# Routing of layer 1's mixture of experts in smaller chunks: eight tiles for the first four, more pieces behind a block, five sends

## The chip, the cores and the metric

The kernel runs on one core of a Trainium2 chip. The metric is the device time of one execution in microseconds; the time before is the median of 3 runs. The core has five engines with queues of their own, each working in order: PE (matmul, with its weight loads shown as PEld), DVE (vector), ACT (activations), POOL (GpSimd) and SP, which here only issues DMAs. POOL issues DMAs too, among them the indirect ones that this change is about.

## The reference, cut to what matters

Four layers, each an attention-like block and a feed-forward block, on 32 x 256 tokens of width 128, that is 8192 tokens, or 64 tiles of 128 tokens. The change lies in layer 1. Its first half is a linear attention with a causal mask; its second half a mixture of eight experts:

```python
x = x + _L1_attn_ref(_layernorm(x), ...)   # q, k, v, gate; elu + 1; causal (q k^T) v / (q . cumsum k)
xf = _layernorm(x).reshape(-1, 128)
logits = xf @ gate_w + gate_b                # (8192, 8)
top_w, top_i = jax.lax.top_k(logits, 2)
gw = softmax(top_w)
out = sum over e of combine[:, e] * (gelu(xf @ w1[e] + b1[e]) @ w2[e] + b2[e])
shared = gelu(xf @ ws1 + bs1) @ ws2 + bs2
x = x + out + shared
```

## The kernel before, in words

The residual stream `K.x` stays in on-chip memory as 64 tiles (`NT`), and a block is four tiles, so there are 16 blocks (`NBLK`). Each token has to reach the two experts that it chose. The kernel does this by sending: the class `Slots` keeps, in device memory, a list of rows for each expert (`f_rows`); every token's normalised row goes, with its return address and its weight, to a slot of the list of its first expert and once more to a slot of its second. Afterwards `S.experts` walks over the lists in groups of 256 rows, fetches a group (`xs<-f_rows`), applies that group's expert and scatters the results back (`f_back`). It can fetch the first group only when all sends have landed.

One send is one indirect DMA from POOL (`S.send`, L478): 128 rows of 130 numbers, one tile for one of the two choices, 128 sends in all. Just before it, DVE casts the tile's slot numbers to integers (`one`, L1422). There are eight buffers of `one`, so a cast waits until the send eight places earlier has landed.

Before a tile can be sent it goes through routing, in chunks of tiles (16 before the change):

- `settle` (L1316): once the attention of the chunk's tiles is done, the mean and the inverse root of the variance are worked out by DVE in small steps (`Norm.steps`, L258 to L300, then L1322), and ACT writes the normalised rows into `row` (L1327), one instruction a tile.
- `gate` (L1333): block by block, PE transposes four tiles of `row`, ACT copies them to `xnT` (L1353), PE multiplies by `gate_w` (L1348), and DVE adds the bias into `logits` (L1359).
- `choose` (L1366): DVE picks the two best experts of each token (L1384 to L1395), ACT takes an exponential, and `Slots.places` works out the slot: the picks are counted by two matmuls (L403 and L404) and one running sum along the tiles of each expert (`tensor_tensor_scan`, L408), whose mask `go_on` starts anew at each expert. At the end two lists of sends are queued in `outgoing`, those of the first choice and those of the second, and between them `second`, which has POOL rewrite the return addresses (L373) and weights (L1417) of the chunk's rows.

`settle` and `choose` are generators: every `yield` ends a piece of one or two instructions. `beside(n, most)` is the call that weaves them in. It issues up to `most` entries of `outgoing` (`send`), runs one `gate`, and then n times advances every active generator by a piece; of the `choose` generators only the first in line advances.

`beside` is called at the end of each round of two loops. The attention's loop has 21 rounds for 16 blocks, in six stages: in round n block n-5 is in `third`, n-4 in `second`, n-3 in `keys`, n-2 in `first`, n-1 in `turn` and n in `scale`; here the call is `beside(10, 5)`. A chunk's `settle` becomes active in the round in which its last block has been through `third`. The shared expert's loop has 17 rounds (`rise`, L1592 and L1596, then `fall` of the block before, L1601, L1607 and L1613), with `beside(14, 4)`. After it everything left in `outgoing` is sent, `S.finish` numbers the groups (L440 to L469), and `S.experts` starts. The experts' weights (`w_all`) are loaded by SP between the two loops.

In both loops the order on PE, ACT and DVE is the order of the program text (`manual_schedule`); POOL's order is left to the scheduler. POOL's other work in the attention is one addition a block (`q+qr`, L1513), whose result `second` reads two rounds later.

The lines in the lists below are those of the kernel before.

Of the kernel before, what the change touches and what calls it, by code (L numbers as in the profile page):

```python
# [11 lines left out]
F32 = mybir.dt.float32  # L12
# [3 lines left out]
ALU = mybir.AluOpType  # L16
# [4 lines left out]
P = 128  # L21
NB, SEQ, D = 32, 256, 128
NT = NB * SEQ // P
# [280 lines left out]
class Slots:  # L304
# [8 lines left out]
    GROUP, WIDE, NE = 256, D + 2, 8  # L313
# [22 lines left out]
            )  # L336
            nc.gpsimd.dma_start(rows[i], t)  # L337

    def begin(self, pool, most):

        nc = self.K.nc
        self.every = pool.tile([P, P], BF16, name="every")
        self.first = pool.tile([P, P], BF16, name="first")
        nc.gpsimd.memset(self.every, 1.0)
        nc.gpsimd.affine_select(
            out=self.first, in_=self.every, pattern=[[1, P]], compare_op=ALU.is_gt, fill=0.0,
            base=0, channel_multiplier=-1,
        )
        self.go_on = pool.tile([P, self.NE, most], F32, name="go_on")
        nc.gpsimd.memset(self.go_on, 1.0)  # L350
        nc.gpsimd.memset(self.go_on[:, :, 0:1], 0.0)
        self.seen = pool.tile([P, self.NE], F32, name="seen")
        self.floor = pool.tile([P, self.NE], F32, name="floor")
        for t in (self.seen, self.floor):
            nc.gpsimd.iota(
                t, pattern=[[self.ROOM, self.NE]], base=0, channel_multiplier=0,
                allow_small_or_imprecise_dtypes=True,
            )
        n = NT * P // self.GROUP
        self.steps = pool.tile([P, n], F32, name="steps")  # L360
# [17 lines left out]
    def places(self, pool, bank, picks, out):  # L378


        NE = self.NE
        nc = self.K.nc
        n, most = picks[0].shape[1], self.go_on.shape[2]

        def new(name, dtype=F32):
            return pool.tile([P, NE * most], dtype, name=name)[:, 0 : NE * n]

        taken = new("taken", BF16).rearrange("p (e n) -> p e n", e=NE)
        turned = [m.rearrange("p n e -> p e n") for m in picks]
        if len(picks) == 1:  # L390
            nc.vector.tensor_copy(taken, turned[0])
        else:
            nc.vector.tensor_add(taken, *turned)
        yield

        yield "PE"
        t = bank()
        before, total = (
            (t[:, i, 0 : NE * n] if len(t.shape) == 3 else t[:, i * NE * n : (i + 1) * NE * n])
            .rearrange("p (e n) -> p e n", e=NE)  # L400
            for i in range(2)
        )
        nc.tensor.matmul(before, self.first, taken, start=True, stop=True)  # L403
        nc.tensor.matmul(total, self.every, taken, start=True, stop=True)  # L404

        sums = new("sums").rearrange("p (e n) -> p e n", e=NE)
        if n == most:
            nc.vector.tensor_tensor_scan(  # L408
                sums.rearrange("p e n -> p (e n)"), self.go_on.rearrange("p e n -> p (e n)"),
                total.rearrange("p e n -> p (e n)"), 0.0, ALU.mult, ALU.add,  # L410
            )
        else:
            for e in range(NE):
                nc.vector.tensor_tensor_scan(
                    sums[:, e, :], self.go_on[:, e, 0:n], total[:, e, :], 0.0, ALU.mult, ALU.add
                )
        slot = new("slot").rearrange("p (e n) -> p e n", e=NE)
        nc.vector.tensor_sub(slot, sums, total)
        nc.vector.tensor_add(slot, slot, before)
        yield  # L420
        nc.vector.tensor_add(slot, slot, self.seen.unsqueeze(2).to_broadcast([P, NE, n]))
        nc.vector.tensor_add(self.seen, self.seen, sums[:, :, n - 1])
        yield
        for m, u in zip(picks, out):
            mine = new("mine").rearrange("p (n e) -> p n e", e=NE)
            s = pool.tile([P, most], F32, name="place")[:, 0:n]
            nc.vector.tensor_mul(mine, m, slot.rearrange("p e n -> p n e"))
            yield
            nc.vector.tensor_reduce(s, mine, axis=AX.X, op=ALU.add)
            yield  # L430
            nc.vector.tensor_copy(u, s)
            yield
# [820 lines left out]
def layer1(K):  # L1253
# [1 line left out]

    nc, ins = K.nc, K.ins
    NE, F = 8, 512
    FC, CHUNK = F // P, 16
    LONG = 2 * F + FC + D
    S = K.slots1  # L1260
    before, after = K.norm_of_x, K.next_norm()
# [10 lines left out]
    with ExitStack() as es:  # L1272
# [13 lines left out]
        gate_b = K.load_bcast(sp, "f1_gate_b", NE)  # L1286
        shared = sp.tile([P, LONG], F32, name="shared")
        numbers(shared, NE, nc.sync)
        S.begin(sp, CHUNK)
        order = sp.tile([P, NE], F32, name="order")  # L1290
        nc.gpsimd.iota(
            order, pattern=[[-1, NE]], base=NE, channel_multiplier=0,
# [22 lines left out]
        active, ready, turned, logits, hold, outgoing = [], [], [], {}, {}, []  # L1315
        slot_of = [rw.tile([P, NT], F32, name=f"slot{i}") for i in range(2)]  # L1316

        def settle(lo):
            hi = lo + CHUNK
            for _ in after.steps(lo, hi):  # L1320
                yield
            nc.vector.scalar_tensor_tensor(  # L1322
                nmr[:, lo:hi], after.mean[:, lo:hi], -1.0, after.r[:, lo:hi], ALU.mult, ALU.mult
            )
            yield
            for j in range(lo, hi):
                nc.scalar.activation(  # L1327
                    row[:, j, 0:D], K.x[:, j, :], AF.Identity, bias=nmr[:, j : j + 1],
                    scale=after.r[:, j : j + 1],
                )  # L1330
                if j % 4 == 3:
                    ready.append(j // 4)
                yield  # L1333

        def gate():

            count = [g for g in active if hold.get(g[1])][:1]
            new = ready.pop(0) if ready else None
# [13 lines left out]
            if new is not None:  # L1352
                nc.scalar.copy(xnT[:, new, :], t)  # L1353
                turned.append(new)
            if old is not None:
                lo, at = 4 * old // CHUNK * CHUNK, 4 * old % CHUNK
                if at == 0:
                    logits[lo] = lw.tile([P, CHUNK, NE], F32, name="lg")
                nc.vector.tensor_add(  # L1359
                    logits[lo][:, at : at + 4, :], out,  # L1360
                    gate_b.unsqueeze(1).to_broadcast([P, 4, NE]),
                )
                if at == CHUNK - 4:
                    active.append((choose(lo), lo))
            for g in count:
                hold[g[1]] = u[:, 256:512]  # L1366
                go(g)

        def choose(lo):
            n, hi = CHUNK, lo + CHUNK  # L1370
            lg = logits.pop(lo)

            def new(name, *shape):
                return rw.tile([P, n, *shape], F32, name=name)

            def wide(t):
                return t.unsqueeze(2).to_broadcast([P, n, NE])
# [87 lines left out]
        with ExitStack() as at:  # L1465
# [79 lines left out]
            def third(blk):  # L1545
# [18 lines left out]
                        ALU.mult, ALU.add,  # L1564
                    )
                after.take(K.x, 4 * blk, 4 * blk + 4)
                if (4 * blk + 4) % CHUNK == 0:
                    active.append((settle(4 * blk + 4 - CHUNK), None))

            with K.tc.manual_schedule(  # L1570
                engines={nc.tensor.engine, nc.scalar.engine, nc.vector.engine}
            ):
                stages = [(5, third), (4, second), (3, keys), (2, first), (1, turn), (0, scale)]
                for n in range(NBLK + 5):
                    for later, stage in stages:
                        if 0 <= n - later < NBLK:
                            stage(n - later)
                    beside(10, 5)


        w_all = K.pool(es, "l1a", 1).tile([P, NE, LONG], F32, name="w_all")
# [2 lines left out]
        with ExitStack() as ps:  # L1584
# [30 lines left out]
            with K.tc.manual_schedule(  # L1615
                engines={nc.tensor.engine, nc.scalar.engine, nc.vector.engine}
            ):
                for n in range(NBLK + 1):
                    if n < NBLK:
                        rise(n)  # L1620
                    if n:
                        fall(n - 1)
                    beside(14, 4)
                assert not (active or ready or turned)
                send(len(outgoing))
                nc.scalar.copy(w_all[:, :, 2 * F + FC :], b2[:, 0:NE, :])
# [1152 lines left out]
```

## Time and profile before

| What | us |
|---|---|
| median of 3 runs (lowest to highest) | 3095.63 (3092.87 to 3099.08) |
| the profiled execution: time / span | 3072.12 / 3070.4 |
| layer 1, attention's rounds with all engines at work | 871 to 991 of the span |
| shared expert's rounds | 991 to 1123 |
| from the last matmul of the shared expert to the first of the experts | 1123 to 1205 |

The profile shows one execution. "Busy" is the time in which an engine had an instruction; an idle engine's waits are named by what ended them. In a list of windows each row is a stretch of the span with the busy time and the number of instructions of each engine, then the clock that PE was granted (1.00 is full) and the share and rate of the DMA engines. In a timeline a row is the start in us, the duration, the engine, line and operation, the output and inputs, and in brackets the idle time before it with what ended it.

### The profile page before, as it was taken

What the parts mean: (1) busy time and instruction counts of PE and PEld (TensorE: products, weight loads), DVE (VectorE), ACT (ScalarE), POOL (GpSimd) and SP (SyncE); (2) the same over time, 40 slices, a digit from 0 to 9 for tenths busy, and PEclk for the clock granted to TensorE, in tenths of its full rate; (3) what the DMA queues carried; (4) which work ended last, traced back from release to release, by engine and by line L of the source; (5) the groups of instructions that cost most, each with busy time, mean ns of one, the idle gap of its engine ahead of it and who ended that gap; (6) DMA issues with size and microseconds to landing.
All of it is one profiled execution on the core that took longest, in us unless ns stands there. A gap on an engine that the chain in (4) does not pass through costs nothing.

```text
span 3070.4 us, 59293 instructions
## 1 busy us (share of the span) xinstructions
PE 2481.3 (81%) x21486; PEld 1840.0 (60%) x21486; DVE 1853.4 (60%) x5498; ACT 1426.3 (46%) x3065; POOL 853.9 (28%) x1235
## 2 busy tenths in 40 slices
PE   4899787899889962999488888996978888887470
PEld 4865444444857742999466667775855555555460
DVE  7215454444878312444379766764869988886447
ACT  3433432222468521444435555556427677776223
POOL 1001444310012455455310101100520223343573
PEclk9999789999989986999779989997979999999795
DMA  2497455540000211222455434430034445451334
GB/s 72 141 283 223 173 231 228 217 152 21 12 1 13 82 40 52 70 70 70 117 155 160 128 113 141 132 95 13 1 86 137 128 125 143 130 147 42 91 91 112
DMA packets 263264, 340.81 MB, mean 111 GB/s; under 512 B 34598, under 2 KB 231062, under 8 KB 254780
## 3 DMA queue, kind: packets, MB, share of 16 engines
q1 hardware_dynamic: 231228, 237.01, 27.1%
q0 software_dynamic: 27584, 97.92, 8.5%
q8 instruction: 170, 2.79, 0.4%
q10 hardware_dynamic: 4160, 2.10, 0.3%
q14 instruction: 122, 1.00, 0.1%
HBM read 156.72 MB, written 177.83 MB: 109 GB/s over the span
## 4 chain that ended last, share of the span: by engine, by line
PE 39%; DVE 12%; DMA 7%; issue 5%; ACT 5%; POOL 4%; SPq 1%; DVEq 0%; POOLq 0%; ACTq 0%
PE o L1909 5%; PE t L1888 5%; DVE top L1845 4%; PE o L557 4%; PE hp L538 4%; DMA q<-row 4%; PE s L1784 2%; PE s L1833 2%; POOL f_back L484 2%; PE d L1607 2%; PE a L1592 2%; ACT e L1896 2%; DMA f_rows<-row,one 2%; DVE st_x L246 1%; PE a L1492 1%
## 5 line engine op out<-in xcount | busy, mean ns | idle before, releaser
L1845 DVE TENSOR_REDUCE top<-s 128x3 f32<-128x384 f32 (+1 forms) x1024 | 600.5, 617 | 189.5 <-PE s L1742 133.3
L1896 ACT ACTIVATE e<-t 128x384 f32<-128x384 f32 (+1 forms) x1024 | 494.0, 546 | 128.2 <-PE s L1742 82.7
L1888 PE MATMUL t<-q,k 64*128 64x256 f32 (+1 forms) x2048 | 417.1, 308 | 115.8 <-ACT e L1896 60.9
L1833 PE MATMUL s<-k,q 48*128 48x256 f32 (+1 forms) x2048 | 437.8, 331 | 30.3 <-DMA k<-d 16.7
L1888 PEld LDWEIGHTS t<-q,k 64*128 64x128 f32 x2048 | 299.7, 191 | 194.8 <-ACT e L1896 90.2
L1833 PEld LDWEIGHTS s<-k,q 48*128 48x128 f32 x2048 | 308.2, 198 | 43.6 <-DVE top L1845 23.9
L544 ACT ACTIVATE h<-hp,w 128x256 f32<-128x256 f32 x368 | 154.6, 471 | 332.8 <-PE hp L538 324.0
L484 POOL DMA_INDIRECT f_back<-y,place x224 | 217.4, 970 | 191.8 <-DVE y L563 125.8
L1909 PE MATMUL o<-e,val 128*32 128x256 f32 (+1 forms) x4096 | 262.0, 376 | 0.0
L538 PE MATMUL hp<-xT,w 128*128 128x256 f32 x736 | 184.4, 390 | 20.4 <-DVE xT L529 20.3
L557 PE MATMUL o<-w,h 128*128 128x128 f32 x1472 | 183.4, 276 | 0.0
L2079 POOL TENSOR_SCALAR xn<-x_sb,mean_x,r_x 128x128 f32<-128x128 f32 x64 | 55.2, 871 | 449.4 <-PE t L1773 394.0
L557 PEld LDWEIGHTS o<-w,h 128*128 128x128 f32 x1472 | 174.0, 193 | 1.5
L1909 PEld LDWEIGHTS o<-e,val 128*32 128x32 f32 x4096 | 110.7, 113 | 81.8 <-issue 12.8
L538 PEld LDWEIGHTS hp<-xT,w 128*128 128x128 f32 x736 | 133.4, 194 | 40.8 <-DVE xT L529 26.4
L1742 PE MATMUL s<-hideq,pick 64*128 64x128 bf16 x1024 | 151.6, 233 | 0.0
L478 POOL DMA_INDIRECT f_rows<-row,one x128 | 123.4, 964 | 94.2 <-DVE one L1422 61.7
L1742 PE MATMUL t<-hidek,pick 64*128 64x128 bf16 x1024 | 147.3, 227 | 0.0
L527 PE MATMUL t<-ident,xs 128*128 128x128 f32 x224 | 43.9, 278 | 101.4 <-DMA xs<-f_rows 101.4
L563 DVE TENSOR_TENSOR y<-o,xs 128x256 f32<-128x256 f32 x112 | 47.3, 422 | 114.2 <-PE o L557 113.9
L337 POOL DMA_DIRECT2D f_rows<-blank x176 | 98.3, 559 | 54.5 <-POOL blank L333 51.2
L775 PE MATMUL up<-wc,hT 128*128 128x128 f32 x768 | 110.8, 297 | 0.0
(522 smaller groups left out, 5294.8 us busy)
## 6 DMA issues: line engine op xcount, KB each, us to landing
f_rows<-blank POOLq DMA_DIRECT2D x176, 390.0 KB, 2.8
tz<-kpad SPq DMA_DIRECT2D x64, 512.0 KB
d<-high SPq DMA_DIRECT2D x128, 256.0 KB
d<-low SPq DMA_DIRECT2D x128, 256.0 KB
q<-d SPq DMA_DIRECT2D x128, 256.0 KB
k<-d SPq DMA_DIRECT2D x128, 256.0 KB
xs<-f_rows SPq DMA_DIRECT2D x112, 130.0 KB
t<-f_back SPq DMA_DIRECT2D x24, 512.0 KB
```

Source lines behind the costliest of these rows:

```text
L478: i = self.K.nc.gpsimd.indirect_dma_start(self.rows, bass.IndirectOffsetOnAxis(ap=slot, axis=0), row, None)
L484: i = self.K.nc.gpsimd.indirect_dma_start(self.back, bass.IndirectOffsetOnAxis(ap=place, axis=0), row, None)
L538: nc.tensor.matmul(hp[:, i, :], w[:, (c + i) * P : (c + i + 1) * P], xT, start=True, stop=True,)
L544: nc.scalar.activation(h[:, c + i, :], hp[:, i, :], act, bias=w[:, b1 : b1 + 1])
L557: nc.tensor.matmul(o[:, i, :], h[:, c, i * P : (i + 1) * P], w[:, F + c * D : F + c * D + D], start=False, stop=i == N - 1 and c == FC - 1,)
L775: nc.tensor.matmul(o, hT[:, 2 * blk + b, s : s + P], wc[:, j, cs], start=j == 0, stop=False)
L1742: nc.tensor.matmul(t.rearrange("p (n q) -> p n q", n=3)[:, 0:3:2, 64 * n : 64 * n + 64], pick[r, n, :], hide[name][r], start=False, stop=n ...
L1833: nc.tensor.matmul(s[:, lo:hi], q[r, p, h * P : (h + 1) * P], k[r, p, 0 : hi - lo], start=h == 0, stop=not causal and h == 1,)
L1845: nc.vector.tensor_reduce(tops[b][:, :, j, p], out_of["s"][:, 0:used].rearrange("q (h k) -> q h k", h=3 if causal else 2), axis=AX.X, op=A ...
L1888: nc.tensor.matmul(t[:, kh * SEQ : kh * SEQ + SEQ - skip], k[r, p, kh * P : (kh + 1) * P], q[r, p, skip:SEQ], start=kh == 0, stop=not caus ...
L1896: nc.scalar.activation(e, t, AF.Exp)
L1909: nc.tensor.matmul(o[32 * i : 32 * i + 32, skip:SEQ], val[b % RING][:, kh, 4 * m + i, 16 * s : 16 * s + 32], e[:, kh * SEQ : kh * SEQ + SE ...
```

## The change

`CHUNKS` takes the place of a fixed `CHUNK`: four chunks of 8 tiles and two of 16. `settle`, `choose` and the bookkeeping of `gate` go by the chunk that a tile belongs to. `Slots.begin` builds a mask `go_on` for each size in use, so that `places` can do one running sum for both sizes. The attention's rounds call `beside(18, 5)` in place of `beside(10, 5)`, and the shared expert's `beside(14, 5)` in place of `beside(14, 4)`. Layer 3 calls `Slots` with a single size, 8, and keeps it.

```diff
-    def begin(self, pool, most):
+    def begin(self, pool, *sizes):
...
-        self.go_on = pool.tile([P, self.NE, most], F32, name="go_on")
-        nc.gpsimd.memset(self.go_on, 1.0)
-        nc.gpsimd.memset(self.go_on[:, :, 0:1], 0.0)
+        self.go_on = {}
+        for n in sizes:
+            go_on = self.go_on[n] = pool.tile([P, self.NE, n], F32, name=f"go_on{n}")
+            nc.gpsimd.memset(go_on, 1.0)
+            nc.gpsimd.memset(go_on[:, :, 0:1], 0.0)
...
-        if n == most:
-            nc.vector.tensor_tensor_scan(
-                sums.rearrange("p e n -> p (e n)"), self.go_on.rearrange("p e n -> p (e n)"),
-                total.rearrange("p e n -> p (e n)"), 0.0, ALU.mult, ALU.add,
-            )
-        else:
-            for e in range(NE):
-                nc.vector.tensor_tensor_scan(
-                    sums[:, e, :], self.go_on[:, e, 0:n], total[:, e, :], 0.0, ALU.mult, ALU.add
-                )
+        nc.vector.tensor_tensor_scan(
+            sums.rearrange("p e n -> p (e n)"), self.go_on[n].rearrange("p e n -> p (e n)"),
+            total.rearrange("p e n -> p (e n)"), 0.0, ALU.mult, ALU.add,
+        )
...
-    FC, CHUNK = F // P, 16
+    FC = F // P
+
+    CHUNKS = [range(lo, lo + 8) for lo in (0, 8, 16, 24)] + [range(32, 48), range(48, NT)]
...
-        S.begin(sp, CHUNK)
+        S.begin(sp, *sorted({len(c) for c in CHUNKS}))
...
+        def chunk_of(j):
+            return next(c for c in CHUNKS if j in c)
+
-        def settle(lo):
-            hi = lo + CHUNK
+        def settle(c):
+            lo, hi = c.start, c.stop
...
-                lo, at = 4 * old // CHUNK * CHUNK, 4 * old % CHUNK
+                c = chunk_of(4 * old)
+                lo, at = c.start, 4 * old - c.start
...
-                if at == CHUNK - 4:
-                    active.append((choose(lo), lo))
+                if at == len(c) - 4:
+                    active.append((choose(c), lo))
...
-                if (4 * blk + 4) % CHUNK == 0:
-                    active.append((settle(4 * blk + 4 - CHUNK), None))
+                c = chunk_of(4 * blk)
+                if 4 * blk + 4 == c.stop:
+                    active.append((settle(c), None))
...
-                    beside(10, 5)
+                    beside(18, 5)
...
-                    beside(14, 4)
+                    beside(14, 5)
```

More of the change, by code (lines that the diff above doesn't have):

```diff
@@ L382, in places @@
         nc = self.K.nc
-        n, most = picks[0].shape[1], self.go_on.shape[2]
+        n, most = picks[0].shape[1], max(self.go_on)
         def new(name, dtype=F32):
@@ L1355, in gate @@
             if old is not None:
-                lo, at = 4 * old // CHUNK * CHUNK, 4 * old % CHUNK
+                c = chunk_of(4 * old)
+                lo, at = c.start, 4 * old - c.start
                 if at == 0:
-                    logits[lo] = lw.tile([P, CHUNK, NE], F32, name="lg")
+                    logits[lo] = lw.tile([P, 16, NE], F32, name="lg")
                 nc.vector.tensor_add(
@@ L1367, in gate, with choose @@
                 go(g)
-        def choose(lo):
-            n, hi = CHUNK, lo + CHUNK
-            lg = logits.pop(lo)
+        def choose(c):
+            lo, hi, n = c.start, c.stop, len(c)
+            lg = logits.pop(lo)[:, 0:n, :]
             def new(name, *shape):
-                return rw.tile([P, n, *shape], F32, name=name)
+                return rw.tile([P, 16, *shape], F32, name=name)[:, 0:n]
             def wide(t):
```

## The prediction

> **What bounds the kernel now.** I read the page's chain first (it names TensorE, PE, for 39% of the span, spread over the whole kernel), then cut layer 1 into stretches. The columns are the stretch, its length, busy time of PE, PEld, DVE, ACT and POOL, granted clock, DMA share and GB/s.
>
> ```profile
> 877.00:985.00 108.00, 103.61 (x617) 80.66 (x616) 96.18 (x348) 91.06 (x170) 18.83 (x14) 0.98 0.00 1
> 1006.50:1123.40 116.90, 116.62 (x713) 87.86 (x711) 29.05 (x133) 54.16 (x86) 54.40 (x60) 1.00 0.15 47
> 1123.40:1202.70 79.30, 0.02 (x1) 0.00 (x0) 14.26 (x72) 0.00 (x0) 56.29 (x63) 0.53 0.15 50
> ```
>
> The first stretch is the attention, where PE, DVE and ACT are all nearly full and POOL has 14 instructions. The second is the shared expert, bound by PE. In the third nothing runs but sends. The waits of that stretch say who pays:
>
> ```profile
> PE t L527 <- DMA xs<-f_rows: 81.7, 1, 81.7
> DVE one L1422 <- DMA f_rows<-row,one: 60.4, 51, 3.3
> ```
>
> PE stands for 81.7 us until the first group of rows can be fetched, which needs every send landed. POOL's timeline prices a send:
>
> ```profile
> 1177.85 0.96 POOL L478 DMA_INDIRECT f_rows<-row,one  x1 [0.30 <-issue]
> 1180.45 0.16 POOL L373 IOTA row<- 128x16 f32 x1 [1.64 <-DMA f_rows<-row,one]
> 1180.54 0.20 POOL L1417 COPY row<-weight 128x16 f32<-128x16 f32 x1
> 1181.23 1.00 POOL L478 DMA_INDIRECT f_rows<-row,one  x1 [0.49 <-POOL row L1417]
> 1182.53 0.96 POOL L478 DMA_INDIRECT f_rows<-row,one  x1 [0.30 <-issue]
> ```
>
> One send every 1.26 us (0.96 + 0.30). The relabelling of the rows for the second choice (`second`, L373 and L1417) waits for sends in flight: 3.38 us from send to send, 3.59 at the other place in this tail, thus 2.2 more than a plain step.
>
> **How many sends go where.** Unrolling both programs (a round is one call of `beside`; rounds 0 to 20 belong to the attention, then 17 to the shared expert): before, 10 sends go out in rounds 19 and 20, 62 in the shared rounds up to the last but one, 56 from the last on. After: 42 in rounds 12 to 20 (5, 4, 5, 5, 5, 4, 5, 5, 4), 77 in the first sixteen shared rounds, 5 in the last and 4 left over, so 9 at the end.
>
> **The tail.** Before, the 56 start from 1126.24 to 1200.28: 53 x 1.263 + 3.59 + 3.38 = 73.9, shown 74.04. After, the last but one round's five may start where its four did (1121.19), the nine follow, and the last starts at 1121.19 + 13 x 1.263 = 1137.6. That is 62.7 us earlier. The expert numbering on DVE (L440 to L469: 1192.48 to 1199.96, 7.5 us) then has less to hide behind: the last cast waits for the ninth send from the end (start 1127.5, landed about 3.3 later), so the numbering ends near 1138.4, before the last send lands at 1139.9. Nothing is added. **-62.7.**
>
> Can POOL hold five per shared round? 6.3 us against rounds of 7.2 us (PE's L1592 x8 3.44 + L1607 x32 3.57 + 0.22): yes, and a round with a `second` (8.5 at most) is caught up in two rounds. The cover is 0.9 us a round; if a send took 1.45 us, POOL would be the bound.
>
> **The attention pays.** Six chunks instead of four are finished earlier, so settling (20 DVE instructions a chunk) and choosing (27) move from the shared rounds, where DVE was busy 29 of 117 us, into rounds where it is nearly full. Plain and loaded blocks of the attention:
>
> ```profile
> 884.51:891.28 6.77, 6.77 (x41) 5.12 (x41) 5.56 (x19) 5.46 (x10) 1.27 (x1) 1.00 0.00 0
> 898.05:906.16 8.11, 8.11 (x47) 6.15 (x47) 7.83 (x30) 6.27 (x11) 1.27 (x1) 1.00 0.00 0
> 936.94:945.60 8.66, 8.66 (x53) 6.64 (x52) 8.28 (x30) 6.18 (x11) 1.27 (x1) 1.00 0.01 2
> ```
>
> A plain block is PE's 6.77 with DVE at 5.56, so DVE hides 1.2 us of extra work, no more; loaded blocks end with DVE 96% busy. Layer 3 already chooses in chunks of 8, so the new size has rows:
>
> ```profile
> L408 DVE TENSOR_TENSOR_SCAN sums<-go_on,s 128x64 f32<-128x64 f32 x8 | 2.3, 286 | 2.5 <-PE s L404 2.5
> L427 DVE TENSOR_TENSOR mine<-pick,slot 128x64 f32<-128x64 f32 x8 | 2.2, 269 | 0.0
> ...
> L418 DVE TENSOR_TENSOR slot<-sums,s 128x64 f32<-128x64 f32 x8 | 1.8, 220 | 0.3
> ...
> L268 DVE SCALAR_TENSOR_TENSOR m_x<-dif_x,m_x 128x8 f32<-128x8 f32 x6 | 0.9, 157 | 0.0
> ```
>
> With the 0.03 to 0.04 between neighbours, settling costs 20 x 0.20 = 4.0 a chunk and choosing about 27 x 0.25 = 6.8 (a chunk of 16 takes 4.2 and 8.2). Casts are 0.08 each (five in 0.39), the gate's addition 0.18. Base per block 5.55, in rounds 16 and 17 4.45 (no scaling). In DVE us by round, from the unrolled counts: round 6 (18 settling pieces) 9.2; 7: 6.0; 8: 9.2; 9: 6.1; 10 (18 + 13 choosing): 12.6; 11: 9.9; 12: 13.0; 13: 10.2; 14: 9.4; 15: 9.9; 16: 12.1; 17: 9.0. Sum 116.6. The same count for before gives 86.7, and its windows show 86.1 busy in 95.1 us. ACT limits rounds 7, 9 and 17 after (8, 8 and 15 rows of 0.40 on top of about 5.5, or 4.5 in round 17): 8.7, 9.2, 10.5. Dividing DVE's rounds by 0.96 and taking ACT's where longer: 127.5. Against 95.1: **+32.4.** From below it is 116.6 - 95.1 = +21.5 (DVE never waits).
>
> **The clock.** PE idles in the heavy rounds. What that may cost:
>
> ```profile
> 978.10:980.30 2.20, 0.00 (x0) 0.00 (x0) 2.13 (x16) 1.65 (x4) 0.00 (x0) 1.00 0.00 0
> 982.00:984.00 2.00, 2.00 (x9) 2.00 (x10) 1.26 (x4) 1.19 (x4) 0.00 (x0) 0.50 0.00 0
> 988.00:990.00 2.00, 2.00 (x20) 2.00 (x19) 1.40 (x10) 1.79 (x5) 1.14 (x2) 1.00 0.00 0
> ```
>
> After 2.2 us without a matmul the clock stood at 0.5 for some 6 us, so one drop costs 3 us of PE work. The Trainium skill, TensorE: Matmul & The Clock Gate, section on HAM oscillation, asks for idle gaps beyond about 3.4 us. My gaps: behind 31 pieces (6.9 us) PE has about 4.9 us left before it needs DVE's next attention outputs (2.4 us later), a gap of 4.4 in rounds 10, 12 and 16: by the page three drops, at most 9 us; by the row (2.2 us is enough) six to eight, 18 to 24. Most lies under DVE, which sets these rounds. I take **+3**, by the page's count and a third of its price; the row's 24 is kept for the range.
>
> **The other moves.** POOL in rounds 12 to 17: five sends 6.3 + L1513 1.3 to 2.1 = 8.4 at most in rounds of 9.8 to 13.5. L1513 (`q+qr`) now queues behind up to five sends; its reader is two rounds later, so nothing. Casts queue ahead of the gate's addition on DVE and wait for the eighth send before (2.3 us to land): covered while POOL keeps up. Rounds 18 to 20 are short (20.8 us together before) and POOL wants 6.3 + 6.3 + 7.3: it just fits. The Trainium skill, SBUF — State Buffer, "SBUF: two separate sides", says that a VectorE instruction in a 2-port mode keeps POOL from writing descriptors. No send of before ran beside the scaling (L139, 4 x 0.34), so no row prices it; by the page at most 4 rounds x 1.37 = 5.5 us of POOL, under a slack of 2 us or so a round: nothing taken.
>
> At the hand-over before, PE's counting matmul (L403) stood behind a cast that waited for a send (995.11 to 1000.35, beside the weight loads), and PE restarted at half clock. After, no count falls in the first shared round; two Exp/Gelu table loads of 1.28 go too. I take **-4**, between -7 (all of it) and +3 (casts wait there instead). One block's transposes and gate matmuls (0.44 + 0.79) leave the PE-bound stage: **-1.2.** The larger scan mask, the scan itself and the set-up move nothing on the path.
>
> **Sum.** -62.7 + 32.4 + 3 - 4 - 1.2 = -32.5. The profiled execution took 3072.1 (span 3070.4), 23.5 below the median 3095.6; I expect 3039.6 for such a one and **3063** as the median.
>
> **Rivals.** (a) The moved work packs better: ACT's 16 rows before cost little in rounds 10 to 12, and DVE may run without gaps: +21.5, no clock loss, -6 at the hand-over: -48, 3047. Against it: the loaded blocks' 4%, and uneven rounds. (b) The gain is half eaten: the row's rule on the clock holds (+21 instead of +3), or sends are slowed beside DVE so that POOL's backlog reaches the end: -32.5 + 18 = -14.5, 3081. For it: the gap of 2.2 us above. This is also the case in which sends leave early in name only. (c) Slower: PE stays at half clock through rounds 10 to 17. A block with a gate is 8.1 us of PE, 16.2 at half, 130 for eight against the 91 in my list: +39, less the 3 taken; the hand-over then starts as cold as before and its 4 are lost: +7.5 in all, 3103. It decides from an average round of 15.3 us on ((91 + 3 + 28.5) / 8). Against it: DVE leaves PE at work for two thirds of each round. (d) No change, 3096: the tail would have to stay though 47 of its 56 sends have left, and no wait in it would hold it.
>
> **Numbers.** Forecast 0.58, (a) 0.2, (b) 0.14, (c) and worse 0.05, (d) 0.03. No change is within 0.2%, 6.2 us, about what this kernel's times resolve. Faster 0.89, same 0.06, slower 0.05. Range 3042 to 3085: from (a) with 5 us over, to (b) with 4.
>
> **What would show it.** The stretch without matmuls before the experts shrinks from 81.7 to about 19 us; POOL's first send comes near 940; rounds 10, 12 and 16 take 12.5 to 13.5 us with DVE over 90% busy; the shared expert keeps 7.2 us a round. I am wrong if the clock stays near 0.5 in the attention, if casts wait long for sends there, or if POOL is far behind when PE ends.

## The result and the profile after

The changed kernel takes **3054.49 us** (median of 4 runs, 3049.28 to 3055.91), the kernel before on the same chip 3094.25 (4 runs, 3083.85 to 3099.08): ratio 0.9876, 95% interval 0.9849 to 0.9903. Forecast were 3063 and 3042 to 3085. It was timed twice more, beside the kernel before each time: 3068.64 to 3100.94 (0.9895, 0.9872 to 0.9917) and 3025.71 to 3066.53 (0.9871, 0.9844 to 0.9897). The kernel's absolute time moves from chip to chip and from one set of timings to the next, so only ratios within one set are compared below. Lines are from here on those of the changed kernel (a send is L474, the cast L1424, the gate's addition L1361, `q+qr` L1515), except for experiments 1 and 3, which start from the kernel before.

The first profile of it (3055.11 us, span 3053.4) has these lines, from the waits of PE and of DVE in the stretch 870 to 1200 and from the list of DMAs:

```profile
PE t L523 <- DMA xs<-f_rows: 26.4, 1, 26.4
```

```profile
DVE x_sb L1616 <- PE a L1595: 22.7, 3, 10.3
```

```profile
f_rows<-row,one POOLq DMA_INDIRECT x128
```

PE's wait ahead of the experts fell from 81.7 to 26.4 us, not to 19. The addition of the shared expert's output (L1616) waited for PE up to 10.3 us, which no profile of before shows. And the line of the sends has no time to landing: this recording kept 21,357 records of landings where the first of before has 26,745. A third profile of the same kernel, taken on another chip, kept them (26,733), and there the same three places read:

```profile
PE t L523 <- DMA xs<-f_rows: 19.1, 1, 19.1
```

```profile
DVE x_sb L1616 <- PE d L1610: 81.9, 16, 7.1
```

```profile
f_rows<-row,one POOLq DMA_INDIRECT x128, 2.3
```

Here no addition waits over 7.1 us, one round of the shared expert. Five of fourteen profiles (the first two of the changed kernel and experiments 4 to 6) lost a fifth of their landing records, and just these five have late PE signals; in each of them layer 1 is worse than the timed runs allow, as the table in the next section shows. I therefore read the changed kernel from its third profile. That the lateness comes from the recording is argued from this agreement, not shown: four of the five were taken on one chip, where before was not profiled, so the chip may have a part in it.

Layer 1 of the third profile, cut as before was: rounds 6 to 17 of the attention; rounds 18 to 20; from the shared expert's first matmul to its first output matmul; the shared expert; the tail up to the experts' first matmul. Columns as in the prediction:

```profile
882.70:1001.30 118.60, 102.43 (x579) 79.00 (x577) 106.63 (x465) 81.84 (x157) 43.87 (x42) 0.94 0.05 15
1001.30:1016.70 15.40, 12.18 (x56) 11.55 (x57) 8.88 (x41) 6.92 (x16) 8.84 (x10) 0.56 0.12 39
1016.70:1025.20 8.50, 8.50 (x31) 4.53 (x31) 3.26 (x26) 4.18 (x6) 4.71 (x5) 1.00 0.87 256
1025.20:1148.10 122.90, 118.80 (x700) 88.48 (x698) 31.84 (x159) 55.13 (x87) 74.81 (x84) 0.97 0.20 62
1148.10:1168.30 20.20, 0.66 (x2) 0.29 (x2) 7.63 (x27) 0.00 (x0) 11.60 (x12) 0.60 0.18 57
```

The same stretches of the kernel before, profiled on the same chip beside it:

```profile
878.20:973.30 95.10, 91.88 (x552) 70.71 (x551) 86.59 (x314) 81.26 (x151) 16.99 (x12) 1.00 0.00 1
973.30:985.30 12.00, 10.63 (x64) 10.21 (x65) 9.35 (x38) 6.86 (x18) 2.42 (x3) 0.72 0.03 10
985.30:1000.60 15.30, 11.01 (x34) 5.45 (x34) 10.41 (x62) 8.14 (x13) 11.49 (x12) 0.78 0.80 233
1000.60:1117.50 116.90, 116.55 (x712) 87.80 (x710) 29.09 (x134) 54.35 (x86) 54.51 (x60) 1.00 0.14 45
1117.50:1200.20 82.70, 0.71 (x3) 0.34 (x3) 14.83 (x74) 0.00 (x0) 56.34 (x62) 0.53 0.16 51
```

Line by line: the attention pays 23.5 us (DVE +20.0 busy, clock 0.94 instead of 1.00), the hand-over (second and third line) gains 3.4, the shared expert pays 6.0, the tail gains 62.5. Sum: **-36.4** (322.0 to 285.6), against 40.8 between the medians of that pair. Three profiles of before put these 322 us within 0.2 of each other, while the rest of the kernel scatters by ten and more between executions; so the experiments are read in these five stretches, and the ratio says whether the whole agrees.

### The profile page after: what moved, and what is told of

It is laid out like the page before. It is cut to its first block, busy times and chain, and to the rows that moved or that the text cites. A ratio compares the mean times of both kernels' runs of the same rounds, so it can differ in the third digit from the quotient of the medians.

```text
span 3053.4 us, 59367 instructions
## 1 busy us (share of the span) xinstructions
PE 2501.0 (82%) x21490; PEld 1854.8 (61%) x21490; DVE 1862.0 (61%) x5592; ACT 1422.0 (47%) x3065; POOL 858.8 (28%) x1243
## 4 chain that ended last, share of the span: by engine, by line
PE 34%; DVE 10%; issue 5%; DMA 4%; ACT 4%; POOL 4%; SPq 1%; ACTq 0%; POOLq 0%; DVEq 0%
PE o L1912 6%; PE t L1891 5%; PE hp L534 4%; PE o L553 4%; DVE top L1848 4%; DMA q<-row 3%; PE s L1787 2%; POOL f_back L480 2%; PE s L1836 2%; ACT e L1899 2%; DVE st_x L246 1%; PE t L1745 1%; PE s L1745 1%; PE s L1931 1%; SPq L1880 1%
## 5 line engine op out<-in xcount | busy, mean ns | idle before, releaser
L474 POOL DMA_INDIRECT f_rows<-row,one x128 | 125.5, 981 | 73.9 <-issue 26.2
L559 DVE TENSOR_TENSOR y<-o,xs 128x256 f32<-128x256 f32 x112 | 47.4, 423 | 128.2 <-PE o L553 106.6
L771 PEld LDWEIGHTS up<-wc,hT 128*128 128x128 f32 x768 | 102.6, 203 | 4.5 <-issue 2.8
```

Source lines behind the costliest of these rows:

```text
L474: i = self.K.nc.gpsimd.indirect_dma_start(self.rows, bass.IndirectOffsetOnAxis(ap=slot, axis=0), row, None)
L771: nc.tensor.matmul(o, hT[:, 2 * blk + b, s : s + P], wc[:, j, cs], start=j == 0, stop=False)
```

## The experiments

All compute the full output. The table has the stretches (us) of each profile, ordered as told below. "Layer 1" is their sum. The last two columns are the differences to before, in layer 1 (to 322) and by the ratio of the timed runs; a star marks the recordings that lost landing records.

| kernel | rounds 6-17 | hand-over | shared | tail | layer 1 | to before, layer 1 | timed |
|---|---|---|---|---|---|---|---|
| before | 95.1 | 27.2 | 116.9 | 82.7 | 322 | | |
| changed, 1st * | 118.9 | 33.9 | 116.6 | 27.6 | 297.0 | -25 | -38 |
| changed, 2nd * | 118.8 | 34.0 | 116.9 | 27.1 | 296.8 | -25 | -33 |
| changed, 3rd | 118.6 | 23.9 | 122.9 | 20.2 | 285.6 | -36 | -40 |
| 1: five sends only | 95.1 | 30.0 | 116.9 | 62.8 | 304.8 | -17 | -16 |
| 2: ten pieces | 103.0 | 20.7 | 127.9 | 40.0 | 291.7 | -30 | -29 |
| 3: chunks of 16 | 109.3 | 31.5 | 117.3 | 43.7 | 301.8 | -20 | -24 |
| 4: no sends in the attention * | 116.3 | 24.0 | 118.2 | 85.3 | 343.8 | +22 | +9 |
| 5: fourteen pieces * | 117.8 | 30.0 | 129.8 | 27.1 | 304.7 | -17 | -23 |
| 6: ten pieces, six sends * | 103.1 | 24.5 | 160.7 | 22.9 | 311.2 | -11 | -27 |
| 7: changed, 16 index tiles | 118.9 | 24.4 | 115.9 | 21.2 | 280.3 | -42 | -41 |
| 8: ten pieces, 16 index tiles | 103.2 | 20.7 | 117.8 | 40.5 | 282.2 | -40 | -45 |

Without a star, the two last columns agree within 5 us. With one, layer 1 comes out 6 to 16 us worse than the timed runs. Of the starred rows I use only rounds 6 to 17, which lie ahead of the late signals and agree with the third profile to 0.3 us for the changed kernel; what else is read from one is marked as not shown.

**Before, again.** Twice, to see the scatter.

> The kernel before, unchanged, a second time. Every theory: no difference, 0 within 6 us of the kernel before. Its profile tells how far the parts of the kernel outside layer 1 differ from one execution to the next: the pair of profiles before and after differs by 24.8 us between the attention's round 6 and the first matmul of the experts, but by 13.9 us the other way behind that. If that 13.9 is scatter, the stretch from the first expert matmul to the end (1864 us in the first profile) is 1870 to 1885 here; if the change causes it, 1864 again.

> The kernel before once more, for its profile on this chip. From round 6 to the experts' first matmul it took 321.8 and 321.9 us in the two profiles so far. If layer 1 is all that the change touches, it takes 321.5 to 322.2 again. The changed kernel and its variants were 5 to 17 us better by the timed runs than by their profiles of layer 1 on the last chip, where PE's signals came late in the records; if that is a matter of the chip or of the recording, this kernel shows late signals there too (additions of the shared expert not 7.2 us apart) and 325 to 335 us in layer 1. Ratio 1.00 within 0.002.

Measured: 3061.94 us, ratio 0.9994 (0.9978 to 1.001), and 3065.97, ratio 0.9998 (0.9977 to 1.002). Layer 1: 321.9 and 322.0, the tail 82.7 both times. On neither chip did a record get lost, so whether a recording with lost landings also lengthens this kernel's layer 1 stays open.

**1. Five sends in the shared expert, nothing else.**

```diff
-                    beside(14, 4)
+                    beside(14, 5)
```

> The kernel before with five sends a round in the shared expert instead of four, and nothing else. Theory (the gain is sends that leave the tail, each worth 1.26 us, and DVE's pieces are the price): the last round and the rest fall from 56 sends with two relabellings to 41 with one, so the stretch without matmuls is 15 x 1.26 + 2.2 = 21 us shorter, the attention is unchanged, and the time is 19 to 21 us below before. Rival (the smaller chunks carry the gain, more sends a round only make POOL late): 0 to -8 us.

Measured: 3046.78 us, ratio 0.9948 (0.9929 to 0.9967). The tail falls by 20 us, close to the 21 expected from 15 sends of 1.26 and one relabelling, and the shared expert stays at 116.9, so POOL holds five sends a round. But the hand-over grows by 2.8, so the whole gains 16 to 17 and not the 19 to 21 expected.

**2. Chunks of 8 with the old ten pieces.**

```diff
 in the changed kernel, attention
-                    beside(18, 5)
+                    beside(10, 5)
```

> The changed kernel with ten pieces a round in the attention, as before, instead of eighteen. 23 sends with one relabelling are left from the last round on (before 56 with two, changed 9). Theory: the tail is 33 x 1.26 + 2.2 = 44 us shorter than before; rounds 6 to 17 hold 176 pieces, against some 120 before and 208 in the changed kernel, so they cost about 15 us where the changed kernel pays 24; with the hand-over's +7 the time is 20 to 26 us below before, so behind the changed kernel by some 15. Rival (pieces cost nothing, DVE has room, and the hand-over sets the loss): 35 us or more below before.

Measured: 3033.31 us, ratio 0.9905 (0.9878 to 0.9932). The tail is as expected (-43). Rounds 6 to 17 cost +7.9 where about 15 were expected, and PE's clock is 1.00 in each of them. The hand-over gains 6.5 instead of losing 7, and the shared expert takes 11 us more, which nobody expected; experiment 8 takes that up. So the whole, -29 to -30, lies between the theory (-20 to -26) and its rival (-35 or more).

**3. The changed counts of pieces and sends, with chunks of 16.**

```diff
 in the kernel before
-                    beside(10, 5)
+                    beside(18, 5)
...
-                    beside(14, 4)
+                    beside(14, 5)
```

> The kernel before with eighteen pieces and five sends, but all chunks of 16 tiles. 26 sends with one relabelling are left from the last round on: the tail is 30 x 1.26 + 2.2 = 40 us shorter. Rounds 6 to 17 hold fewer pieces than before (97 against 120), since settling and choosing of the first two chunks are all that falls there; they cost 0 to 5 us more than before (bunched pieces, ten sends), the hand-over up to 7. Theory: 28 to 38 us below before, as good as the changed kernel within 8 us. Rival (small chunks are needed for the gain): 20 us below before or less.

Measured: 3038.89 us, ratio 0.9923 (0.99 to 0.9947). The tail is as expected (-39), the attention is not: +14.2 in rounds 6 to 17 instead of 0 to 5. Two of its rounds say why:

```profile
913.30:926.02 12.72, 8.05 (x37) 6.67 (x36) 5.74 (x19) 12.66 (x28) 1.27 (x1) 0.73 0.01 2
951.41:966.93 15.52, 11.76 (x54) 9.58 (x53) 9.35 (x33) 12.21 (x28) 1.27 (x1) 0.78 0.00 0
```

In both ACT is busy 12.2 to 12.7 us with 28 instructions against 10 in a plain block: the 18 pieces let ACT scale a chunk of 16 in one round, so here ACT sets the round while DVE has room. The clock fell in both (0.73, 0.78). With chunks of 8 a round gets 8 rows at once (until the first chunk of 16, in round 17). Small chunks do not merely bring the first send forward, they cap what ACT gets at once. Without them 20 us of gain remain in layer 1 and 24 by the timed runs, at or above the rival's 20 and short of the theory's 28 to 38.

**The changed kernel, again.**

> The changed kernel, unchanged, a second time, on the chip of the experiments. In its first profile DVE and ACT got PE's signals 3 to 7 us late at four places (hand-over and three late rounds of the shared expert), which no other profile shows. If that belongs to the change, layer 1 takes 297 us again from round 6 to the experts' first matmul, hand-over 18 us, tail 27.6. If it belongs to that execution alone, the hand-over is about 4 us shorter and the tail about 7 (20 us), so layer 1 about 287 and the time some 34 us below before, not 25.

> The changed kernel once more. If the late PE signals in three rounds of its shared expert belong to its program, they come back at the same rounds, with a tail of 27 to 28 us and 297 us in layer 1. If they belong to the chip or the recording, and are absent here, the additions are 7.2 us apart and the tail is 20 to 21 us as predicted, layer 1 289 to 291. Ratio to before 0.987 to 0.990 in either case.

Measured: ratios 0.9895 and 0.9871 as above. The second profile repeats the first (late signals at the same rounds, tail 27.1), the third has neither: tail 20.2, additions 7.2 us apart. So the lateness is not a property of the program alone.

**4. No sends in the attention.**

```diff
 in the changed kernel, attention
-                    beside(18, 5)
+                    beside(18, 0)
```

> The changed kernel with no sends in the attention's rounds (they go out later, so the output is complete): 52 sends with two relabellings are left from the last round on, so the tail is as long as before less 5 us, about 78. It tells whether rounds 6 to 17 cost 24 us for the moved pieces or for the sends. Theory (pieces on a full DVE): rounds 6 to 17 take 115 to 118 us where the changed kernel takes 118.9, since only 28 casts of 0.08 us go. Rival (sends: casts wait, POOL and DVE share a port): 108 or less. Hand-over: theory of late casts says 15 or less in place of 18, and rounds 18 to 20 12 in place of 15.9. In all some 15 us slower than before.

Measured: 3108.73 us, ratio 1.0029 (1.0016 to 1.0042): all the routing work moved forward, and nothing gained from it (the tail of 85.3 is from a starred recording). Rounds 6 to 17 take 116.3 us without sends and 118.6 to 118.9 with 28 of them. So of the attention's price of 23.5 the sends make 2.3 to 2.6, and the routing work the other 21.

**5. Fourteen pieces.**

```diff
 in the changed kernel, attention
-                    beside(18, 5)
+                    beside(14, 5)
```

> The changed kernel with 14 pieces a round in the attention in place of 18: the same number of pieces in the attention (221 against 224 in rounds 6 to 19), the same sends at the same rounds, 9 left at the end, only spread more evenly: at most 28 pieces in a round instead of 32. Theory A (DVE's total sets rounds 6 to 17): 118 us again, the time equal to the changed kernel within 4 us. Theory B (the bunches leave PE idle, its clock falls, and this is part of the 24): 108 to 113 us, and 6 to 10 us faster than the changed kernel.

Measured: 3079.21 us, ratio 0.9925 (0.9896 to 0.9955). Rounds 6 to 17 take 117.8 us, nearly as with 18 pieces. Unrolled, both issue 208 instructions of settling and choosing on DVE in these rounds, and both make the first sends in round 12; with ten pieces it is 163, first sends in round 15. So between 14 and 18 it is not how many pieces stand behind one block that sets the price, but how many have been done by round 17. The time is 10.6 us above that of the changed kernel timed beside it, where theory A had 4 at most, though the two intervals overlap; the starred profile has the shared expert 13 us longer, which is not shown to be the cause.

**6. Ten pieces, six sends in the shared expert.**

```diff
 in the changed kernel
-                    beside(18, 5)
+                    beside(10, 5)
...
-                    beside(14, 5)
+                    beside(14, 6)
```

> Ten pieces in the attention, as in the second experiment (23 sends left, layer 1 at 291.7 us), and six sends a round in the shared expert: 6 + 2 sends left at the end. POOL's six take 7.58 us against rounds of 7.22, so it falls behind by 0.4 us a round and 2.2 at each relabelling, some 11 us by the end of the last eleven rounds. Theory (POOL's total sets the end): tail 40 - 15 x 1.26 + 5 to 11 = 26 to 32 us, layer 1 278 to 284, 38 to 44 us below before and the fastest so far. Rival (POOL late holds up DVE's casts and so PE): the shared expert longer by more than 5 us and no gain over five.

Measured: 3073.58 us, ratio 0.9914 (0.9892 to 0.9935). In the waits of DVE from 999 to 1190:

```profile
DVE one L1424 <- DMA f_rows<-row,one: 16.9, 16, 2.3
```

Expected were 38 to 44 us below before; the timed runs give 27. Casts wait 16 times in this recording, and six sends are 7.6 us of POOL against rounds of 7.2, which fits the rival (POOL late holds up the casts). But the stretch of 160.7 us is longer than this makes it (17 rounds x 0.4 = 7), and the recording is one of the starred, so the cause is not shown. What the timed runs show is that nothing is gained over the changed kernel timed beside it (0.9895) or over five sends (experiment 2, 0.9905).

**7 and 8. Sixteen index tiles for sends instead of eight.**

```diff
-                one = lw.tile([P, 1], mybir.dt.uint32, name=f"one{j % 4}")
+                one = lw.tile([P, 1], mybir.dt.uint32, name=f"one{j % 8}")
```

Experiment 7 is the changed kernel with this, 8 has `beside(10, 5)` in the attention as well.

> The changed kernel with 16 index tiles for the sends in flight instead of 8, so that a cast on DVE waits for the sixteenth send before it and not for the eighth. Theory: the hand-over (rounds 18 to 20 and the shared expert's first round) costs 7 us more than before because casts wait there and hold the gate's addition, the counting matmul and so PE; then its 33.9 us fall to 24 to 27 (24.0 were measured without any send in the attention), layer 1 to 287 to 291 (7 less again if no PE signal is late), ratio to the changed kernel 0.997. Rival: the weight loads or PE's signals hold it, not the casts: 33 to 35 us stay. In rounds 6 to 17 no cast waited, so 118.8 us stay by both.

> The changed kernel with 10 pieces behind a block instead of 18 and 16 index tiles instead of 8. With 10 pieces and 8 tiles the shared expert took 127.9 us, 11 over its 116.8, and layer 1 291.7. Theory: those 11 us are casts that wait for sends ahead of the gate's addition; the shared expert falls to 117 to 120 and layer 1 to 281 to 284, which is 13 to 16 below the changed kernel and a ratio to it of about 0.995. Rival, as for the other run: 127 to 129 and 291 to 293 stay. Tail: 19 sends are left over with both, about 40 us.

Measured: 3024.21 us, ratio 0.9866 (0.9842 to 0.9889), and 3020.66, ratio 0.9854 (0.9831 to 0.9878), beside 3025.71 of the changed kernel (3015.84 to 3035.93): both are faster than before, and not to be told from the changed kernel by the timed runs. In layer 1 they are, by one profile each: 280.3 and 282.2 against 285.6.

For 8 the theory held: the shared expert falls from 127.9 to 117.8. With eight tiles (experiment 2) casts waited up to 3.96 us there, ACT then 8.15 us for `e` and PE 6.98 us for `h`; with sixteen no cast waits before the tail, and both gaps are gone. For 7 the place was wrong. The hand-over was 23.9 already in the undisturbed profile; what the tiles bring is in the shared expert, 122.9 to 115.9. (The first two profiles of the changed kernel, both starred, also have 116.6 and 116.9 there, but with a hand-over of 34; hand-over and shared expert together are 150.5, 150.9 and 146.8 with eight tiles and 140.3 with sixteen.) There the chain can be followed. DVE's timeline of the changed kernel, third profile (start, duration, instruction, idle time before it):

```profile
1019.19 0.15 DVE L1424 CAST one<-slot 128x1 uint32<-128x1 f32 x1 [0.84 <-DMA f_rows<-row,one]
...
1022.40 0.15 DVE L1424 CAST one<-slot 128x1 uint32<-128x1 f32 x1 [2.89 <-DMA f_rows<-row,one]
...
1024.11 0.15 DVE L1424 CAST one<-slot 128x1 uint32<-128x1 f32 x1 [1.38 <-DMA f_rows<-row,one]
...
1027.14 0.17 DVE L1323 SCALAR_TENSOR_TENSOR nmr<-mean_x,r_x 128x16 f32<-128x16 f32 x1
```

ACT and then PE of the same profile:

```profile
1027.35 4.72 ACT L1328 ACTIVATE row<-x_sb,nmr,r_x 128x128 f32<-128x128 f32 x12 [5.18 <-DVE nmr L1323]
1031.98 2.39 ACT L1599 ACTIVATE h<-a,shared 128x512 f32<-128x512 f32 x4
```

```profile
1032.70 1.12 PE L146 MATMUL a<-ident,row 128*128 128x128 f32 x4 [3.75 <-ACT h L1599]
1033.61 1.72 PE L1349 MATMUL d<-w_f_gate_w,xnT 128*128 128x8 f32 x8
1035.17 5.83 PE L1595 MATMUL a<-xnT,shared 128*128 128x512 f32 x8
```

Beside the weight loads the sends land 4.6 to 5.0 us after their issue (those of 1017 to 1023) instead of 2.3, and the cast that reuses such a send's index tile waits: 5.1 us in these three. The settling pieces queue behind the casts, so `nmr` is late, ACT stands 5.18 us for it and then scales twelve rows ahead of `h`, PE waits 3.75 us for `h` and restarts at half clock (L1595 5.83 instead of 3.68). In experiment 7 sends still take up to 5.3 us, but with 16 tiles no cast waits for them, and the same instructions read:

```profile
1022.06 4.73 ACT L1328 ACTIVATE row<-x_sb,nmr,r_x 128x128 f32<-128x128 f32 x12 [1.57 <-DVE nmr L1323]
1026.69 2.39 ACT L1599 ACTIVATE h<-a,shared 128x512 f32<-128x512 f32 x4
```

```profile
1027.41 0.66 PE L146 MATMUL a<-ident,row 128*128 128x128 f32 x4
1027.91 0.96 PE L1349 MATMUL d<-w_f_gate_w,xnT 128*128 128x8 f32 x8
1028.72 3.68 PE L1595 MATMUL a<-xnT,shared 128*128 128x512 f32 x8
```

## Why the prediction was right, step by step

Forecast and measured change per stretch, third profile against before (us):

| step | forecast | measured |
|---|---|---|
| tail | -62.7 | -62.5 |
| attention, DVE's and ACT's rounds | +32.4 | +23.5, clock and sends within |
| attention, clock | +3 | in the line above |
| hand-over | -4 | -3.4 |
| shared expert (one block's gate) | -1.2 | +6.0 |
| sum | -32.5 | -36.4 |

The forecast sum is within 4 us of the measured one partly by luck: the attention was priced 12 too dear and the shared expert 7 too cheap.

**The tail held**, mechanism and size, in this profile; in the first two, whose signals are late up to its start, it fell by 55. Its last sends, on POOL's timeline of the third profile:

```profile
1148.31 0.95 POOL L474 DMA_INDIRECT f_rows<-row,one  x1 [0.30 <-issue]
1149.57 0.96 POOL L474 DMA_INDIRECT f_rows<-row,one  x1 [0.30 <-issue]
...
1160.93 1.07 POOL L474 DMA_INDIRECT f_rows<-row,one  x1 [0.30 <-issue]
1162.30 0.95 POOL L474 DMA_INDIRECT f_rows<-row,one  x1 [0.30 <-DVE start L465]
```

PE ends at 1148.10; twelve sends, 1.26 to 1.27 apart, are left, the nine counted and three of the round before them. The numbering of the experts (L465 is in it) ends beside them, as said, and PE's wait is 19.1 us against the forecast 19. That POOL can hold five in 7.2 us is shown by experiment 1.

**The attention was the step that was mis-sized**, by 12 us of 35: 10 of them in DVE's own work, 2 in its idle time.

*DVE's sum.* I counted 116.6 us in rounds 6 to 17, 106.6 were busy. Rounds 6 to 9 agree (counted 9.2, 6.0, 9.2, 6.1; busy 9.17, 6.46, 9.34, 5.71). Most of the excess (7.2 of 10.0) is in the three rounds with settling and choosing at once: round 10 was 12.6 against 10.59, round 12 13.0 against 10.32, round 16 12.1 against 9.55. DVE's timeline of round 10:

```profile
925.89 0.22 DVE L1386 TENSOR_REDUCE m<-lg 128x8 f32<-128x64 f32 x1
926.02 0.16 DVE L273 TENSOR_SCALAR v_x<-m_x 128x8 f32<-128x8 f32 x1
926.14 0.23 DVE L1388 TENSOR_TENSOR eq<-lg,m 128x64 f32<-128x64 f32 x1
926.28 0.17 DVE L280 TENSOR_SCALAR t_x<-v_x 128x16 int32<-128x16 int32 x1
926.40 0.22 DVE L1390 TENSOR_TENSOR eq<-eq,order 128x64 f32<-128x64 f32 x1
...
927.73 0.17 DVE L292 SCALAR_TENSOR_TENSOR r_x<-u_x,r_x 128x16 f32<-128x16 f32 x1
927.94 0.17 DVE L294 TENSOR_TENSOR t_x<-r_x 128x16 f32<-128x16 f32 x1
928.15 0.18 DVE L296 TENSOR_TENSOR t_x<-t_x,v_x 128x16 f32<-128x16 f32 x1
```

The two generators take turns, so neighbours do not depend on each other, and each starts before the one before has ended: a pair takes 0.26 us (two in 925.89 to 926.40), though its rows say 0.22 and 0.16. Settling alone, each on the result of the last, takes 0.21 a piece (927.73 to 927.94). I had priced each piece as in a chain, with 0.03 to 0.04 behind it, 0.20 and 0.25, thus 0.45 a pair.

*Idle DVE and the clock.* This term was nearly right in size and wrong in place. The forecast left DVE 10.9 us idle (127.5 less 116.6) and 3 more for the clock; it was idle for 12.0 (118.6 less 106.6). But the forecast had ACT limit rounds 7, 9 and 17, and DVE rounds 10, 12 and 16. Rounds 8 and 12:

```profile
899.02:910.60 11.58, 10.01 (x53) 6.84 (x52) 9.34 (x37) 11.30 (x23) 1.27 (x1) 1.00 0.00 0
938.88:951.14 12.26, 12.26 (x64) 8.92 (x63) 10.32 (x56) 8.57 (x17) 4.88 (x5) 0.93 0.06 18
```

ACT fills round 8 (DVE idle for 2.2 us, in rounds 7 and 9 for 0.1 each), and PE fills round 12, as it does 14 and 16, where DVE is idle for 1.2 to 1.9 us. Each of these three follows a round in which PE had a gap, at the gate's counting matmul:

```profile
935.06 0.21 PE L405 MATMUL d<-taken,first 128*128 128x64 bf16 x1 [3.68 <-DVE lg L1361]
957.54 0.19 PE L405 MATMUL d<-taken,first 128*128 128x64 bf16 x1 [3.44 <-DVE lg L1361]
978.69 0.21 PE L405 MATMUL d<-taken,first 128*128 128x64 bf16 x1 [2.99 <-DVE lg L1361]
```

This wait I did not name: the matmul waits for the gate's addition of its round, and that addition stands on DVE behind the pieces of the round before and its own round's attention work. It comes once each in rounds 11, 13 and 15, and each time the clock drops. In all three the scaling just ahead of the addition took 2.05 to 2.06 us instead of 1.11 beside POOL's `q+qr` (last section), so some 0.95 us of each gap is not due to the pieces. In steps of 2 us, around the first:

```profile
932.00:934.00 2.00, 0.00 (x0) 0.00 (x0) 2.00 (x3) 1.19 (x3) 2.00 (x1) 0.93 0.00 0
934.00:936.00 2.00, 0.94 (x6) 0.94 (x6) 1.57 (x8) 0.00 (x0) 0.06 (x1) 0.50 0.00 0
936.00:938.00 2.00, 2.00 (x11) 2.00 (x11) 1.83 (x12) 1.26 (x4) 0.00 (x0) 0.50 0.00 0
938.00:940.00 2.00, 2.00 (x8) 1.64 (x7) 1.86 (x11) 2.00 (x6) 0.00 (x0) 0.50 0.00 0
940.00:942.00 2.00, 2.00 (x7) 1.24 (x6) 2.00 (x8) 1.53 (x3) 0.00 (x0) 0.87 0.00 0
```

Three gaps and three drops were forecast, in rounds 10, 12 and 16, by the limit of 3.4 us that the Trainium skill, TensorE: Matmul & The Clock Gate, gives in its section on HAM oscillation; three there are, but in rounds 11, 13 and 15 and by the wait just named, so the count is right by luck. They lasted 6.8, 3.4 and 3.4 us at half speed, some 7 us of PE's work together, where at most 9 were allowed. The limit itself does not hold here: the gap of 2.99 us drops the clock too, as before's 2.2 did, and the measurement decides (the last section has more). What the drops cost by themselves no run separates: with ten pieces (experiment 2) the clock is 1.00 in all rounds and DVE idles 4.5 us instead of 12.0, but 45 instructions are moved out of these rounds as well (8.0 us of DVE's busy time), and the two together give the 15.5 us between 103.0 and 118.6.

The lower bound, +21.5, was nearly the truth by luck, because the 10.0 counted too much and the 12.0 of idle time that it leaves out nearly cancel: 106.6 + 12.0 is 2 above the 116.6 counted as if DVE never waited.

**The hand-over held**, -3.4 for -4, against first appearance: the first two profiles show +6.6, and experiment 1, which has the old chunks, +2.8. That casts wait there (the bound of +3) is real with chunks of 16: in experiment 1 the gate's addition L1359 kept PE 5.53 us from its counting matmul, behind a cast. With chunks of 8 no count falls there, as forecast.

**The shared expert did not keep its 7.2 us a round at once**: +6.0 for -1.2. The forecast said that casts cost nothing while POOL keeps up. They wait for landings, and beside the weight loads landings are late though POOL issues a send every 1.27 us; experiments 7 and 8 show the chain and its price by their profiles, 7 and 10 us. From the eighth round on the pitch is 7.2, as before.

**Other points.** No send ran beside the scaling, and the median send in the attention took 0.962 us (0.955 to 1.081), as in the shared expert, so the rule on descriptors was left untested. The first send came at 941 in the first profile and 946.6 in the third, whose round 6 began 4 us later. Rounds 10, 12 and 16 took 12.5, 12.3 and 10.9 us with DVE busy for 84 to 88%, not over 90%: in 12 and 16 PE was the busier one, and in 10 too (11.83 of 12.49).

**Against the rivals.** (a), 3047, is as near the measured 3054 as the forecast 3063 is, and its +21.5 for the attention nearer than the forecast's 35. Its reason was half true: the moved work does pack better, but DVE does wait and the clock does fall. (b) is out, since POOL is not behind and sends are not slowed. (c) would need PE at half clock through rounds 10 to 17; the stretch has 0.94. (d) is out by 62.5 us of tail. Experiment 4 shows how the change could have been slower: the work brought forward without the sends.

## What to carry to other kernels

When work is moved off an idle tail into a full stretch, price it by the chain it runs in: two independent chains taken in turns took 0.26 us a pair on DVE where their rows add up to 0.38 and two chains by themselves to more, and look what stands on DVE in front of the next thing that PE needs, for that is where PE's gaps came from. Size a ring of index tiles for transfers by their slowest landing, not their average one; by the profiles here, eight tiles cost 7 to 10 us just where weights were loading and landings took 5 us instead of 2.3. And before a new wait is explained, look whether the recording is whole: three additions up to 10 us late were not there in a profile of the same kernel that had lost no records.

## What the hardware showed that was not expected

- In round 10 DVE started an independent small instruction 0.12 to 0.14 us after the last, and in settling alone a dependent one about 0.21 us after (rows above, durations 0.16 to 0.23).
- The length of a gap does not by itself decide whether PE's clock falls. It fell to 0.5 with gaps of 3.68, 3.44, 2.99 and 2.5 us (third profile) and before's 2.2, and stayed 1.00 after 1.57 and 1.38. But in the third profile, ahead of round 6, 2.91 us left it at 1.00, and experiment 8 lost it for 3.4 us after 1.83, where 1.82 at the same place in experiment 2 had left it at 1.00:

```profile
863.92 2.41 PE L1494 MATMUL a<-xnT,w_a_w 128*128 128x512 f32 x5 [2.91 <-ACT xnT L1484]
864.00:866.00 2.00, 2.00 (x5) 0.97 (x6) 0.69 (x1) 1.76 (x4) 0.11 (x1) 1.00 0.00 0
...
945.30 0.19 PE L405 MATMUL d<-taken,first 128*128 128x64 bf16 x1 [1.83 <-DVE lg L1361]
946.50:948.50 2.00, 2.00 (x9) 1.81 (x9) 1.97 (x18) 0.00 (x0) 0.00 (x0) 0.50 0.00 0
```

- POOL's addition `q+qr` (L1515) and DVE's scaling (L139) slow each other: four scalings took 2.05 to 2.06 us instead of 1.11 all three times they met it, and it took 2.37, 2.40 and 1.42 instead of 1.27 (third profile, 931.69, 953.89 and 975.96). A settling instruction of 0.16 us that met it (L260 at 923.62) took 1.08 and ended with it, at 924.70 against 924.67. That agrees with the Trainium skill, SBUF — State Buffer, "SBUF: two separate sides", by which DVE and POOL take a shared pair of ports in turn; its other half, that DVE holds back descriptors, no run here shows.
